# A graph layer on one core: edge products on 64 rows of the array in steps of four tiles, with the older setup, in place of products on 128 rows in steps of two

## The chip, the core and the metric

The kernel runs on one core of one Trainium2 chip. Its time is the time of one execution on the device in microseconds (us); the median of several runs is given. Five engines work side by side, each on its own queue in order: TensorE (PE, with its weight loads shown apart as PEld), VectorE (DVE), ScalarE (ACT), GpSimd (POOL, here used to issue indirect DMAs) and SyncE (SP, which issues DMAs).

## What is computed

There are 12,500 nodes with 128 features and 412,500 edges with 64 features, sorted by `dst`. With `h = relu(layernorm(x))`:

```python
h0 = h @ Wn + bn;  q = h @ Wq + bq;  k = h @ Wk + bk;  v = h @ Wv + bv
eh = edge_features @ We + be
hmid = leaky_relu(concat(q[src], k[dst], eh) @ A1 + b1, 0.2)
scores = leaky_relu(hmid @ A2 + b2, 0.2)
w = softmax(scores.mean(-1), over all edges)
out = segment_sum(w[:, None] * v[dst], src)
result = x + gamma * layernorm(h0 + out) + beta
```

## The kernel before

`A1` is folded into the weights of q, k and the edges at the start (L261 to L266), so that an edge's hidden row is a sum of three rows of 128 numbers. Edges are handled in tiles of 128; eight tiles are a group (`SUPER`), and there are 403 groups.

**Setup** (L171 to L594). The index lists `src` and `dst` are read by SP at once (L246, L248) into a pool of their own; `indices()` (L293) makes from them, on DVE, the place of each edge's source node, its block and its offset in a window of 42 nodes, and writes the offsets to DRAM (`off_d`), eight columns of tiles with one copy and one DMA (L346, L347). `nodes()` (L545) goes over the 98 node tiles in 20 groups of five: layer norm, transpose, one product with four weights into a bank, then three bf16 parts of q, k and v. The remainders between the parts are formed in PSUM, by a product with minus the identity (L579, L581). Beside it run the count of edges per block (`count`, L380) and 98 DMAs that clear the ends of the first table (`clear_ends`, L161). In all of the setup SP's queue goes in the program's order (L243); the other engines' order is the scheduler's.

**First stage** (`first_stage`, L652). For each tile it makes the rows of 128 edges: the product of the edge features with `w_ea`, and, summed into the same bank, the k and v rows of the window, picked by a 0/1 matrix `sel` made on DVE (L678). The edge features of a group come with the features of tiles 0 to 3 on partitions 0 to 63 and those of tiles 4 to 7 on partitions 64 to 127. Before the change `w_ea` is a block matrix of 128 rows and 2 x 128 columns, zero off the diagonal, so that one f32 product of 128 rows (L700) gives the edge part of tile k and of tile k+4, side by side in one bank; two bf16 products (L703) add the window's rows. One step does two tiles; a `Later` object puts off the bank's eviction by one step: ACT copies the place (L683) and the bank (L686, 128x512) into a row tile, and POOL scatters its two tiles with two indirect DMAs (L642) into a table in DRAM, ordered by the blocks of the source. PSUM has two banks for this (`ps_row`), the row tiles are seven buffers (`pr`).

**Second stage** (`second_stage`, L713). For each block of 128 source nodes it reads the block's rows back (L723), turns them on PE (L759), adds q with another 0/1 matrix (L762), takes the leaky maximum (L770 on ACT, L771 on DVE), makes scores (L779, L786, L790, L796, L808 to L831), and sums the weighted v rows on PE (L854) into `acc` (L861, L863). Its jobs stand in a plan written out by hand: each is put at a step with a fixed lag to the one that it needs.

The edges go in four chunks of 86, 121, 121 and 75 groups. While chunk c is in the first stage, chunk c-1 is in the second, the slots of chunk c+1 are worked out (`ready`: `count`, `plan`, `place_slots`, the last with the chain PE L475, DVE L519) and the table of c+1 is cleared. `interleave` takes the next step of whichever job is furthest behind, and the queues of PE, DVE, ACT and SP keep this order in the main loop (L1021). A group counts as four steps of the first stage before and after the change.

Of the kernel before, what the change touches and what calls it, by code (L numbers as in the profile page):

```python
# [10 lines left out]
FP = mybir.dt.float32  # L11
# [11 lines left out]
P = 128  # L23
# [33 lines left out]
def _ceil(a, b):  # L57
    return -(-a // b)
# [21 lines left out]
class Later:  # L80


    def __init__(self):
        self.now = 0
        self.todo = {}

    def after(self, steps, job):
        self.todo.setdefault(self.now + steps, []).append(job)

    def step(self):  # L90

        self.now += 1
        for job in self.todo.pop(self.now, []):
            job()

    def rest(self):
        while self.todo:
            self.step()
            yield


@with_exitstack
def kernel(ctx: ExitStack, tc: tile.TileContext, n_edges, x, src, dst, ea, w_nv, w_qt, w_kt,
# [71 lines left out]
    minus_b = const.tile([P, P], BF, name="minus_b")  # L175
    nc.vector.tensor_scalar(minus_b, ident, -1.0, None, op0=ALU.mult)
# [54 lines left out]
    w_ea = const.tile([P, 2, D], FP, name="w_ea")  # L231
# [11 lines left out]
    early.enter_context(tc.manual_schedule(engines={ET.SP}))  # L243
    xp = early.enter_context(tc.tile_pool(name="index", bufs=1))
    raw_src = xp.tile([P, NT], I32, name="raw_src")
    nc.sync.dma_start(out=raw_src, in_=src)  # L246
    raw_dst = xp.tile([P, NT], I32, name="raw_dst")
    nc.sync.dma_start(out=raw_dst, in_=dst)  # L248
    nc.vector.memset(w_ea, 0.0)

    with tc.tile_pool(name="prep", bufs=1) as prep, tc.tile_pool(name="prep_ps", bufs=1, space=PSUM) as pps:
# [13 lines left out]
        for b in range(2):  # L265
            nc.vector.tensor_copy(w_ea[b * DE:(b + 1) * DE, b, :], fold[b * DE:(b + 1) * DE, 2, :])  # L266
# [22 lines left out]
    np_ = early.enter_context(tc.tile_pool(name="nodes", bufs=2))  # L289
    tps = early.enter_context(tc.tile_pool(name="t_ps", bufs=2, space=PSUM))  # L290
    mps = early.enter_context(tc.tile_pool(name="m_ps", bufs=4, space=PSUM))

    def indices():  # L293
        f = xp.tile([P, NT], FP, name="f")
        nc.vector.tensor_copy(f, raw_src)
# [9 lines left out]
        nc.vector.scalar_tensor_tensor(raw_src, f, float(P), whole, op0=ALU.mult, op1=ALU.add)  # L305
        nc.scalar.dma_start(out=qrow_d, in_=raw_src)

        if t_end < NT:
# [3 lines left out]

        offset = xp.tile([P, NT], FP, name="offset")
        nc.vector.tensor_copy(offset, raw_dst)
# [4 lines left out]
        nc.tensor.matmul(t_bank[:, :NG], lhsT=ones[0:1, :], rhs=head, start=True, stop=True)  # L319
        nc.vector.tensor_sub(offset.rearrange("p (g k) -> p g k", k=SUPER),  # L320
                             offset.rearrange("p (g k) -> p g k", k=SUPER),
                             t_bank[:, :NG].unsqueeze(2).to_broadcast([P, NG, SUPER]))
# [13 lines left out]
        off_t = xp.tile([P, _ceil(NT, P), P], U8, name="off_t")  # L336
        for t0 in range(0, NT, 8 * P):
            m = min(8 * P, NT - t0)
            off_ps = tps.tile([P, 8, P], BF, name="tp")
            for j in range(_ceil(m, P)):  # L340
                w = min(P, m - j * P)
                nc.tensor.transpose(off_ps[:w, j, :], off_b[:, t0 + j * P:t0 + j * P + w], ident_b)
            j0 = t0 // P
            j = m // P
            if j > 0:
                nc.vector.tensor_copy(off_t[:, j0:j0 + j, :], off_ps[:, 0:j, :])  # L346
                nc.scalar.dma_start(out=off_d[t0:t0 + j * P, :].rearrange("(j p) e -> p j e", p=P),  # L347
                                    in_=off_t[:, j0:j0 + j, :])
            if m > j * P:
                w = m - j * P  # L350
                nc.vector.tensor_copy(off_t[:w, j0 + j, :], off_ps[:w, j, :])
                nc.scalar.dma_start(out=off_d[t0 + j * P:t0 + m, :], in_=off_t[:w, j0 + j, :])

    indices()
# [190 lines left out]
    def nodes():  # L545
        for t0 in range(0, NTN, NGRP):
# [5 lines left out]
            parts = np_.tile([P, NGRP, 3, D], BF, name="parts")  # L552
            parts2 = np_.tile([P, NGRP, 3, 2 * D], BF, name="parts2")
            for j0 in range(0, n, 4):
# [6 lines left out]
                for i in range(0, m, 2):  # L561
                    two = range(i, min(i + 2, m))
                    mp = {}
                    for j in two:
                        mp[j] = mps.tile([P, 4, D], FP, name="mp")
                        nc.tensor.matmul(mp[j].rearrange("p a d -> p (a d)"), lhsT=hT[:, j, :],
                                         rhs=w_all.rearrange("p a d -> p (a d)"), start=True, stop=False,
                                         skip_group_check=True)
                    for j in two:
                        nc.vector.tensor_add(mp[j][:, 1:4:2, :], mp[j][:, 1:4:2, :], bias_all[:, 1:4:2, :])  # L570
                        nc.vector.tensor_add(hn[:, j0 + j, :], mp[j][:, 0, :], bias_all[:, 0, :])

                    for s in range(3):
                        for j in two:
                            q, kv = parts[:, j0 + j, s, :], parts2[:, j0 + j, s, :]
                            nc.scalar.activation(kv, mp[j][:, 2:4, :], AF.Copy)
                            if s < 2:
# [74 lines left out]
    def first_stage(c):  # L652
# [28 lines left out]
        def evict(g, k, bank):  # L681
# [5 lines left out]
            for b in range(2):  # L687
                scatter(c, g, b * halves + k, row[:, b, :], sent)
# [400 lines left out]
```

## Time and profile before

| | us |
|---|---|
| median of 3 runs (6614.16 to 6650.77) | 6635.68 |
| the profiled execution's own time | 6635.68 |
| its span, from the first to the last instruction | 6634.0 |
| setup, up to the first scatter | 372 |
| chunk 0 in the first stage | 372 to 1395 |
| chunk 1 in the first stage | 1395 to 2962 |
| chunk 2 in the first stage | 2962 to 4603 |
| chunk 3 in the first stage | 4603 to 5722 |
| second stage alone | 5722 to 6490 |
| sums, layer norm, output | 6490 to 6634 |

The boundaries of the chunks are the starts of their first scatters on POOL. In the profile's rows a matmul's duration includes its way through the array, so that the matmuls of one run overlap: what one costs a full queue is the distance from one start to the next. An f32 product stands in the rows as two records, each with a weight load of its own.

### The profile page before, as it was taken

To read this page: it belongs to the slowest core of one execution; us is meant where nothing else is said; L and a number is where in the kernel's file an instruction comes from. 1 tells how busy PE (TensorE), PEld (TensorE's weight loads), DVE (VectorE), ACT (ScalarE), POOL (GpSimd) and SP (SyncE) were. 2 spreads that over 40 slices of the span, in tenths; PEclk is the share of its full clock that TensorE was granted. 3 is DMA by queue.
4 is the path that set the end of the run, shared out by engine and by line. 5 is a ranking of instruction groups with operands and counts; after the bars stand their busy time and mean duration, and the time that the engine had idled before them with its cause. 6 is when DMAs were issued, how large, how long until landed. Compare 5 with 4: busy or idle time off the path is not lost. (4 is left out here: it accounts for less than half of the span.)

```text
span 6634.0 us, 100311 instructions
## 1 busy us (share of the span) xinstructions
PE 5220.0 (79%) x32180; PEld 3524.0 (53%) x32180; DVE 4479.1 (68%) x14096; ACT 2187.9 (33%) x5896; POOL 3379.4 (51%) x3236
## 2 busy tenths in 40 slices
PE   5666655568888887878888888887999999988881
PEld 3333433245555555556556555555676767665550
DVE  8655655556666666667666666665777777777778
ACT  3432222223333333333333333333343434333331
POOL 0057677765666666656666665565555555200000
PEclk8777677778989889889999998888999999999995
DMA  6755454557777777767777777676777878544443
GB/s 191 215 169 158 136 160 153 157 183 205 221 216 222 220 214 221 218 203 230 242 246 242 238 235 229 218 230 210 247 257 254 256 257 259 186 152 152 153 141 117
DMA packets 607567, 1362.17 MB, mean 205 GB/s; under 512 B 120100, under 2 KB 336860, under 8 KB 569016
## 3 DMA queue, kind: packets, MB, share of 16 engines
q1 hardware_dynamic: 423572, 880.87, 46.3%
q0 software_dynamic: 154704, 424.26, 17.7%
q10 hardware_dynamic: 28756, 50.57, 2.4%
q8 instruction: 255, 4.18, 0.3%
q14 instruction: 280, 2.29, 0.1%
HBM read 782.14 MB, written 573.14 MB: 204 GB/s over the span
## 5 line engine op out<-in xcount | busy, mean ns | idle before, releaser
L642 POOL DMA_INDIRECT tab<-row,slots x3223 | 3377.7, 1048 | 2341.8 <-issue 807.8
L686 ACT ACTIVATE row<-row_ps 128x512 f32<-128x512 f32 x1612 | 952.3, 591 | 1421.6 <-PE row_ps L703 607.7
L700 PE MATMUL row_ps<-w_ea,ea_t 128*128 128x256 f32 x3224 | 1111.5, 430 | 121.9 <-ACT row L686 71.8
L854 PE MATMUL o_ps<-rows_of,w 128*128 128x128 f32 x7252 | 1121.3, 298 | 71.7 <-DVE w L845 48.9
L771 DVE TENSOR_TENSOR rows_of<-h_ps,low 128x512 f32<-128x512 f32 (+1 forms) x980 | 634.9, 648 | 652.9 <-ACT low L770 412.7
L845 DVE TENSOR_SCALAR w<-iota_f,rows_of,score 128x128 f32<-128x128 f32 x3626 | 1022.4, 351 | 10.6
L854 PEld LDWEIGHTS o_ps<-rows_of,w 128*128 128x128 f32 x7252 | 941.9, 199 | 119.6 <-DVE w L845 73.8
L770 ACT ACTIVATE low<-h_ps 128x512 f32<-128x512 f32 (+1 forms) x980 | 551.2, 562 | 1115.6 <-PE h_ps L762 496.0
L700 PEld LDWEIGHTS row_ps<-w_ea,ea_t 128*128 128x128 f32 x3224 | 623.6, 213 | 492.3 <-issue 205.7
L762 PE MATMUL h_ps<-sel_q,qw 128*128 128x512 bf16 (+1 forms) x2940 | 774.8, 373 | 4.6 <-DVE sel_q L750 3.3
L519 DVE TENSOR_REDUCE num<-run 128x5 f32<-128x500 f32 x646 | 433.4, 671 | 402.9 <-remote 212.9
L703 PE MATMUL row_ps<-kv,sel 126*128 126x256 bf16 x3224 | 679.3, 295 | 12.3 <-DVE sel L678 11.7
L779 PE MATMUL s_ps<-rows_of,a_sb 128*32 128x512 f32 (+1 forms) x1960 | 513.8, 625 | 126.3 <-DVE most_of L826 55.3
L759 PE MATMUL h_ps<-ident,rows_of 128*128 128x128 f32 x3626 | 589.3, 284 | 0.5 <-issue 0.5
L475 PE MATMUL run<-one,rest_b 128*128 128x500 f16 x642 | 275.3, 429 | 317.0 <-DVE num L519 240.5
L759 PEld LDWEIGHTS h_ps<-ident,rows_of 128*128 128x128 f32 x3626 | 449.7, 147 | 108.5 <-issue 83.3
L703 PEld LDWEIGHTS <-sel 126*128 126x128 bf16 x3224 | 344.0, 107 | 304.2 <-issue 73.4
L796 PEld LDWEIGHTS s_ps<-heads,z 96*128 96x128 f32 (+1 forms) x3136 | 389.3, 193 | 199.9 <-DVE z L790 142.4
L796 PE MATMUL s_ps<-heads,z 96*128 96x3 f32 (+1 forms) x3136 | 409.0, 251 | 90.8 <-DVE z L790 73.0
L786 ACT ACTIVATE z<-s_ps,b_col 64x512 f32<-64x512 f32 (+1 forms) x392 | 267.4, 682 | 615.1 <-PE s_ps L779 418.5
L468 DVE TENSOR_TENSOR one<-bins_b,block 128x500 f16<-128x500 bf16 x646 | 430.9, 667 | 0.3 <-PE run L475 0.3
L790 DVE SCALAR_TENSOR_TENSOR z<-z 64x512 f32<-64x512 f32 (+1 forms) x392 | 267.4, 682 | 203.5 <-ACT z L786 178.4
(178 smaller groups left out, 4929.0 us busy)
## 6 DMA issues: line engine op xcount, KB each, us to landing
rows_of<-tab SPq DMA_DIRECT2D x196, 1413.5 KB
ea_t<-in_ea SPq DMA_DIRECT2D x403, 256.0 KB
tab<-blank SPq DMA_DIRECT2D x392, 257.0 KB
rows_of<-tab SPq DMA_DIRECT2D x98, 1028.0 KB
rows_of<-tab SPq DMA_DIRECT2D x98, 899.5 KB
tab<-row,slots POOLq DMA_INDIRECT x3223
offs<-off_d SPq DMA_DIRECT2D x403, 126.0 KB
qw<-q_tab SPq DMA_DIRECT2D x392, 96.0 KB
```

What stands on the lines that cost most here:

```text
L642: i = nc.gpsimd.indirect_dma_start(out=tabs[c][:, :], out_offset=bass.IndirectOffsetOnAxis(ap=slots[c][t // (8 * STR)][:m, t % (8 * STR):t ...
L686: nc.scalar.activation(row[:, :, 1:ROW], bank, AF.Copy)
L700: nc.tensor.matmul(bank[:, :, 0:D], lhsT=ea_g[:, ts(k, P)], rhs=w_ea, start=True, stop=False, skip_group_check=True)
L703: nc.tensor.matmul(bank[:, b, :], lhsT=sel[:, ts(b * halves + k, P)], rhs=kv, start=False, stop=True, skip_group_check=True)
L759: nc.tensor.matmul(h_ps[:, ts(j, P)], lhsT=rows_of[i][:, q * QUAD + j, 1:D + 1], rhs=ident, is_transpose=True, start=j == 0, stop=False, s ...
L762: nc.tensor.matmul(h_ps[:, 0:m * P], lhsT=qws[i][:, ts(k, D)], rhs=plss[i][:, q * QUAD * P:(q * QUAD + m) * P], start=False, stop=k == 2, ...
L770: nc.scalar.activation(low, h_ps, AF.Copy, scale=SLOPE)
L771: nc.vector.tensor_max(rows_of[i][:, q * QUAD:q * QUAD + m, 1:D + 1], h_ps.rearrange("p (j e) -> p j e", j=m), low.rearrange("p (j e) -> p ...
L779: nc.tensor.matmul(state["s_ps"][32 * q:32 * (q + 1), 0:m * P], lhsT=a2_sb, rhs=rows_of[i][:, q * QUAD:q * QUAD + m, 1:D + 1], start=True, ...
L796: nc.tensor.matmul(state["s_ps"][:, 0:nq * QUAD].rearrange("p (q j) -> p j q", j=QUAD)[:, j, :], lhsT=state["z"][:32 * nq, ts(j, P)], rhs= ...
L845: nc.vector.tensor_scalar(w, iota_f, rows_of[i][:, t, 0:1], state["score", i][:, t:t + 1], op0=ALU.is_equal, op1=ALU.mult)
L854: nc.tensor.matmul(state["o_ps"][:, 0:D], lhsT=w, rhs=rows_of[i][:, t, D + 1:ROW], start=t == 0, stop=t == ct - 1)
```

## The change

Two parts of the kernel change together.

In the first stage the weights are one matrix of 128 columns again, on both halves of the partitions, and each tile has an f32 product of its own on 64 rows: tiles k and k+1 on the array's rows 0 to 63 into one bank, tiles k+4 and k+5 on rows 64 to 127 into the other. A step does four tiles, a `yield` follows, the two banks are evicted, and another `yield` follows. The `Later` class goes.

The setup is another one. SP's queue is left to the scheduler. `src` and `dst` are read by ACT's queue, one after the other, into one buffer in a pool that opens only when the folding of the weights is done, and that closes before the nodes' pools open. The offsets go out with one copy and one DMA for each 128 tiles. The remainders of the bf16 parts are formed in SBUF, by DVE subtractions over five tiles at a time, and ACT makes all parts. `acc` is cleared with a memset, and the first chunk adds to it in place of a copy.

```diff
-    w_ea = const.tile([P, 2, D], FP, name="w_ea")
+    w_ea = const.tile([P, D], FP, name="w_ea")
...
-    early.enter_context(tc.manual_schedule(engines={ET.SP}))
-    xp = early.enter_context(tc.tile_pool(name="index", bufs=1))
-    raw_src = xp.tile([P, NT], I32, name="raw_src")
-    nc.sync.dma_start(out=raw_src, in_=src)
-    raw_dst = xp.tile([P, NT], I32, name="raw_dst")
-    nc.sync.dma_start(out=raw_dst, in_=dst)
-    nc.vector.memset(w_ea, 0.0)
...
-        for b in range(2):
-            nc.vector.tensor_copy(w_ea[b * DE:(b + 1) * DE, b, :], fold[b * DE:(b + 1) * DE, 2, :])
+        nc.vector.tensor_copy(w_ea, fold[:, 2, :])
...
-    np_ = early.enter_context(tc.tile_pool(name="nodes", bufs=2))
-    tps = early.enter_context(tc.tile_pool(name="t_ps", bufs=2, space=PSUM))
-    mps = early.enter_context(tc.tile_pool(name="m_ps", bufs=4, space=PSUM))
-
-    def indices():
+    with tc.tile_pool(name="index", bufs=1) as xp, tc.tile_pool(name="index_ps", bufs=1, space=PSUM) as ips:
+        raw = xp.tile([P, NT], I32, name="raw")
+        nc.scalar.dma_start(out=raw, in_=src)
...
+        raw = xp.tile([P, NT], I32, name="raw")
+        nc.scalar.dma_start(out=raw, in_=dst)
...
-            if j > 0:
-                nc.vector.tensor_copy(off_t[:, j0:j0 + j, :], off_ps[:, 0:j, :])
-                nc.scalar.dma_start(out=off_d[t0:t0 + j * P, :].rearrange("(j p) e -> p j e", p=P),
-                                    in_=off_t[:, j0:j0 + j, :])
...
+                nc.vector.tensor_copy(off_t[:w, j, :], off_ps[:w, j, :])
+                nc.scalar.dma_start(out=off_d[t0 + j * P:t0 + j * P + w, :], in_=off_t[:w, j, :])
...
-                        for j in two:
-                            q, kv = parts[:, j0 + j, s, :], parts2[:, j0 + j, s, :]
-                            nc.scalar.activation(kv, mp[j][:, 2:4, :], AF.Copy)
-                            if s < 2:
-                                nc.vector.tensor_copy(q, mp[j][:, 1, :])
-                                nc.tensor.matmul(mp[j][:, 2:4, :], lhsT=minus_b, rhs=kv, start=False, stop=False,
-                                                 skip_group_check=True)
...
+                    nc.vector.tensor_add(hn[:, j0 + j, :], mp[:, 0, :], bias_all[:, 0, :])
+                    nc.vector.tensor_add(qkv[:, j0 + j, :].rearrange("p (a d) -> p a d", a=3),
+                                         mp[:, 1:4, :], bias_all[:, 1:4, :])
...
+            for s in range(3):
+                for to, of in ((parts, qkv[:, :n, 0:D]), (parts2, qkv[:, :n, D:3 * D])):
+                    if s < 2:
+                        nc.scalar.activation(to[:, :n, s, :], of, AF.Copy)
+                        nc.vector.tensor_sub(of, of, to[:, :n, s, :])
...
-    acc = ctx.enter_context(tc.tile_pool(name="acc", bufs=1)).tile([P, NTN, D], FP, name="acc")
+    acc = late.tile([P, NTN, D], FP, name="acc")
+    nc.vector.memset(acc, 0.0)
...
         for g in range(g0, g0 + n):
-            for k in range(halves):
-                later.step()
+            for k in range(0, halves, 2):
 
                 ea_g, kv, sel = got[g]
-                bank = ps_row.tile([P, 2, 2 * D], FP, name="row_ps")
-                nc.tensor.matmul(bank[:, :, 0:D], lhsT=ea_g[:, ts(k, P)], rhs=w_ea, start=True, stop=False,
-                                 skip_group_check=True)
+                banks = [ps_row.tile([P, 2, 2 * D], FP, name="row_ps") for _ in range(2)]
+                for j in range(2):
+                    for b in range(2):
+                        nc.tensor.matmul(banks[b][:, j, 0:D], lhsT=ea_g[b * DE:(b + 1) * DE, ts(k + j, P)],
+                                         rhs=w_ea[b * DE:(b + 1) * DE, :], start=j == 0, stop=False,
+                                         skip_group_check=True)
                 for b in range(2):
-                    nc.tensor.matmul(bank[:, b, :], lhsT=sel[:, ts(b * halves + k, P)], rhs=kv, start=False, stop=True,
-                                     skip_group_check=True)
-                later.after(1, lambda g=g, k=k, bank=bank: evict(g, k, bank))
+                    for j in range(2):
+                        nc.tensor.matmul(banks[b][:, j, :], lhsT=sel[:, ts(b * halves + k + j, P)], rhs=kv, start=False,
+                                         stop=True, skip_group_check=True)
                 if k == 0 and g + 2 < g0 + n:
                     load(g + 2)
-                if k == 1 and g + 1 < g0 + n:
+                yield
+                for b in range(2):
+                    evict(g, b * halves + k, banks[b])
+                if k == 0 and g + 1 < g0 + n:
                     select(g + 1)
                 yield
...
-            if c == 0:
-                nc.vector.tensor_copy(acc[:, b, :], state["o_ps"][:, 0:D])
-            else:
-                nc.vector.scalar_tensor_tensor(acc[:, b, :], acc[:, b, :], score[:, ct:ct + 1], state["o_ps"][:, 0:D],
-                                               op0=ALU.mult, op1=ALU.add)
+            nc.vector.scalar_tensor_tensor(acc[:, b, :], acc[:, b, :], state.pop(("score", i))[:, ct:ct + 1],
+                                           state["o_ps"][:, 0:D], op0=ALU.mult, op1=ALU.add)
```

## The prediction

> **What bounds the kernel now.** I read the page first, then the busy time by stage (boundaries: the first scatter of each chunk), then PE's timeline, then the waits.
>
> ```profile
> PE 5220.0 (79%) x32180; PEld 3524.0 (53%) x32180; DVE 4479.1 (68%) x14096; ACT 2187.9 (33%) x5896; POOL 3379.4 (51%) x3236
> ...
> L642 POOL DMA_INDIRECT tab<-row,slots x3223 | 3377.7, 1048 | 2341.8 <-issue 807.8
> L686 ACT ACTIVATE row<-row_ps 128x512 f32<-128x512 f32 x1612 | 952.3, 591 | 1421.6 <-PE row_ps L703 607.7
> L700 PE MATMUL row_ps<-w_ea,ea_t 128*128 128x256 f32 x3224 | 1111.5, 430 | 121.9 <-ACT row L686 71.8
> ...
> L703 PE MATMUL row_ps<-kv,sel 126*128 126x256 bf16 x3224 | 679.3, 295 | 12.3 <-DVE sel L678 11.7
> ```
>
> PE is the busiest engine, and the changed product (L700) is one of its two largest lines. ACT waits mostly for PE's L703, POOL mostly for its own issuing. By stage (columns: stretch, length, busy us of PE, PEld, DVE, ACT, POOL with counts, granted clock, DMA share, GB/s):
>
> ```profile
> 0.00:372.00 372.00, 230.37 (x1457) 121.74 (x1458) 272.71 (x875) 144.75 (x476) 1.70 (x13) 0.84 0.71 203
> 372.00:1395.00 1023.00, 616.96 (x3007) 339.75 (x3007) 600.40 (x1662) 239.69 (x691) 718.15 (x688) 0.72 0.50 154
> 1395.00:2962.00 1567.00, 1269.21 (x7606) 857.97 (x7606) 1005.84 (x3242) 528.81 (x1446) 1003.67 (x969) 0.87 0.73 215
> 2962.00:4603.00 1641.00, 1359.01 (x8637) 960.18 (x8636) 1058.21 (x3327) 573.95 (x1555) 1014.52 (x969) 0.92 0.74 231
> 4603.00:5722.00 1119.00, 1069.31 (x7119) 783.55 (x7116) 816.76 (x2636) 446.28 (x1190) 641.38 (x599) 0.99 0.79 251
> ```
>
> A scatter costs POOL 1048 ns and 251 ns of issue (807.8 us / 3223), 1.30 us. In chunk 0 that is 688 x 1.30 = 894 of 1023 us: **POOL paces it**. In chunk 3 PE is busy 1069 of 1119 us: **PE paces it**. Between them no engine is full. A busy PE counts overlapping records, so I also summed the records at their start-to-start distances and divided by the granted clock: PE's real work is 52, 71, 74 and 85% of chunks 0 to 3. The rest is waiting in a chain of engines with fixed lags.
>
> **The products, per four tiles.** At full clock L700's two records start 215 ns apart and L703's 108 (medians of start times, 1700 to 2600 and 4300 to 6500 us). Now: 2 x (2 x 215 + 2 x 108) = 1292 ns. After: four f32 products of 128 columns are eight records; records of that size (L854, 128x128 f32) start 112 ns apart. Whether the two halves of the array run beside each other is the main question. No row of before shows two row groups in turn, but two show parts of it.
>
> ```profile
> 1909.82 0.38 PE L703 MATMUL row_ps<-kv,sel 126*128 126x256 bf16 x2
> 1910.13 1.05 PE L796 MATMUL s_ps<-heads,z 64*128 64x2 f32 x8
> 1911.12 1.16 PE L854 MATMUL o_ps<-rows_of,w 128*128 128x128 f32 x8
> ```
> ```profile
> 4822.62 1.06 PE L779 MATMUL s_ps<-rows_of,a_sb 128*32 128x512 f32 x6
> 4823.61 0.29 PE L730 MATMUL t_bank<-ident,rows_of 128*11 128x128 f32 x1
> ```
>
> The second: three f32 products into different column strips, two of 512 columns and one of 384. At L700's price (215 ns for 256 columns of a record) they cost 4 x 430 + 2 x 323 = 2.37 us one after the other; the next group starts after 0.99 us. So f32 products on separate parts of the array **do overlap** here. The first prices going into a 64-row form and out: from L703 to a 64-row L796 200 ns, to a 96-row one 108; out to L854 177 against 111. That is 92 + 66 = 158 ns per visit.
>
> On this the Trainium skill, "TensorEngine Tiling (Array Packing)", Key Properties, speaks against the change: "Changing tiling mode (not just tile) drains the TensorE". The trace agrees, with the 158 ns above. By "TensorE: Matmul & The Clock Gate", Part 3, row tiles start about 4 ns apart, so that a pair would take one product's time: the overlapping sum below.
>
> - Overlapping: 92 + 4 x 111 + 66 + 4 x 108 = **1034 ns**, 258 less.
> - One after the other: 92 + 8 x 111 + 66 + 4 x 108 = **1478 ns**, 186 more.
>
> By chunk there are 172, 242, 242 and 150 steps of four tiles at clocks 0.72, 0.87, 0.92, 0.99. Overlapping, PE is spared 62 + 72 + 68 + 39 = 240 us; otherwise it pays 44 + 52 + 49 + 28 = 173. I take overlapping, since L779 is the nearest row. How much reaches the end I choose by stage: 0.15 where POOL paces, 0.35, 0.35, and 0.7 where PE does: 9 + 25 + 24 + 27 = **-85 us**. What is late next is POOL (3224 x 1.30 = 4190 of the first stage's 5350 us) and the second stage's chain with DVE.
>
> **The banks.** Each pair of banks is filled, evicted in the next half step and filled again: the distance is as before, but ACT now makes two evictions in it. The second comes 0.2 (L683, 195 ns) + 0.6 (L686) = 0.8 us later, and behind a waiting product stands all of PE's queue. Between the end of an eviction and the load of L700 that reuses its bank two steps on, the slack is 2.0 us at the median in chunk 0, 3.0 in chunks 1 and 2, 3.6 in chunk 3; about one in ten is under 0.8. The mean of what 0.8 exceeds the slack by is 41 ns; x 806 steps = **+33 us**. If a wait of that kind held nobody up, 0; if every step paid 0.8, 645.
>
> **Bursts.** Every other step gets 1034 ns of PE for 646, the one between gets none, with two evictions and four scatters (5.2 us of POOL, where a step lasts 3.0 to 3.8). Seven row buffers of two tiles cover POOL. PE's 0.39 us is the risk: answers in the second stage's chain (L796, L813, L820 with DVE between) come later in even steps. Bounds: 0 if the slack takes it up, 806 x 0.39 = 313 if every even step grows and no odd one shrinks. With a median slack of some 3 us I choose under a quarter: **+70 us**.
>
> **The setup**, up to 372 us. Removed in L700's line: only the memset of the block matrix (0.27 us). The index lists: `raw_src` and `raw_dst` are issued at 0.8 and 9.0 us and cast at 9 and 16; after, they wait for the folding's buffers (last reader L272, ending at 22.5 us, earlier without the lists ahead of it), and the second for the first's cast. The index work on DVE, which ends at 57 us, ends some 10 to 30 us later, plus 26 copies of 0.27 us for 4.0 us (+3). DMAs: 26 in place of 5 to `off_d` on ACT's queue at 0.4 us, with one buffer reused four times. Nodes per group of five on DVE: out go 5 x (L570 429 + two L578 of 284 - a 128x384 addition of 560, from L361's 128x384) = 2.2 us; in come subtractions of 640 and 1280 columns, twice each, 2 x (0.81 + 1.46) = 4.5 us, by L361's 815 ns for 640 and its slope of 1.0 ns per column; net +2.3 us, 20 groups: +47 us of DVE, which is busy 273 of 372. PE loses the minus-identity products; ACT's copies stay about as many elements. The DMA share is 0.7 to 0.8 there, so the bytes, which are the same, can hide part. SP's queue without a told order can put the 98 clearing DMAs ahead of node loads; bound 0 to 30. The memset of `acc` (at most 13.2 us, L919's row for that size) finds DVE idle before the lists land: 0, else 13. `acc`'s first sums grow by 57 ns x 98 = 6 us of DVE, busy 64% there: 0. Sum of the bounds: 0 to 120; I take 30 for the lists and 20 of the 47: **+50 us**.
>
> **The sum**, against the profiled execution's 6635.7 (1.7 around its span; it is the median too): 6635.7 - 85 + 33 + 70 + 50 = **6704 us**, +1.0%.
>
> **Rivals.**
> 1. *Faster.* PE paces all chunks: 0.7 of the 240 us counts, the bursts vanish in the slack, the setup costs half: 6635.7 - 168 + 33 + 25 = **6526**. For it: PE over 80% busy from chunk 1 on. Against: POOL at 87% in chunk 0, real work of PE near 72% in chunks 1 and 2. With the other terms as forecast (33 + 70 + 50 = 153 us) it decides from 153 / 240 = 0.64 of the spared time on.
> 2. *The halves don't overlap.* Then PE pays; of the 173 us I count 0.3, 0.5, 0.5, 0.8: +86. 6635.7 + 86 + 33 + 70 + 50 = **6875**. For it: no row with two row groups. Against: L779.
> 3. *The setup grows* to +110, DVE being full and SP's order poor, the rest as forecast: **6764**.
>
> **Chances.** Forecast (6640 to 6770) 0.42, rival 1 0.22, rival 2 0.20, rival 3 0.16. The range leaves out the lower half of rival 1 and the upper part of rival 2, about 0.2: 6540 to 6900. A measurement can tell about 0.5% (33 us) from no change; below 6602 lie 0.20 of rival 1 and 0.03 of the forecast, within 0.12 in all, above 6669 the rest: 0.23, 0.12, 0.65.
>
> **What would show it.** The 64-row records of the two halves starting a few ns apart, and four tiles in about 1.03 us of PE (1.48: rival 2). Waits of the products for L686 growing from 217 us. The first scatter near 420 us. Chunk 3 shorter, chunk 0 not. Wrong would be a first scatter by 380, or chunk 1 and 2 shorter by over 60 us each (rival 1).

## The result, and the profile after

The changed kernel takes **6944.37 us** (median of 4 runs, 6935.73 to 6959.5) beside 6633.55 us of the kernel before (4 runs, 6614.16 to 6650.77): a ratio of **1.0472**, interval [1.0435, 1.0508]. It is slower by 311 us, where 68 were forecast: 174 us above the forecast's own range (6640 to 6770 us), and 44 above the wider one that takes in the rivals (6540 to 6900). Its profiled execution took 6936.2 us with a span of 6934.5 us.

The page of the changed kernel, the lines that answer to those of before:

```profile
PE 5230.4 (75%) x35012; PEld 3411.6 (49%) x35012; DVE 4550.3 (66%) x13999; ACT 2163.0 (31%) x5624; POOL 3357.4 (48%) x3236
...
L597 POOL DMA_INDIRECT tab<-row,slots x3223 | 3355.7, 1041 | 2643.0 <-ACT row L638 904.2
L639 ACT ACTIVATE row<-row_ps 128x512 f32<-128x512 f32 x1612 | 944.2, 590 | 1462.6 <-PE row_ps L659 523.3
...
L654 PE MATMUL row_ps<-w_ea,ea_t 64*128 64x128 f32 x6448 | 724.2, 343 | 86.7 <-ACT row L639 43.6
...
L659 PE MATMUL row_ps<-kv,sel 126*128 126x256 bf16 x3224 | 580.9, 311 | 17.8 <-DMA offs<-off_d 15.1
```

The edge product's busy time fell from 1111.5 to 724.2 us, though it has twice the instructions. Single scatters and evictions cost what they did. What grew is POOL's idle time, 2341.8 to 2643.0 us, and its chief releaser is now ScalarE's row (95 us of the growth are the longer wait for the first scatter). By stage, cut again at the first scatter of each chunk (columns as in the prediction's table):

```profile
0.00:485.00 485.00, 187.93 (x1073) 92.95 (x1074) 337.36 (x778) 146.36 (x205) 1.75 (x13) 0.84 0.61 156
485.00:1552.00 1067.00, 625.36 (x3689) 318.05 (x3687) 601.08 (x1665) 223.80 (x690) 717.54 (x689) 0.65 0.47 147
1552.00:3175.00 1623.00, 1283.18 (x8583) 832.01 (x8583) 1008.00 (x3239) 525.59 (x1446) 1006.44 (x968) 0.83 0.69 208
3175.00:4857.00 1682.00, 1379.19 (x9607) 950.35 (x9605) 1058.33 (x3324) 566.31 (x1554) 1008.09 (x968) 0.89 0.72 226
4857.00:6018.00 1161.00, 1074.42 (x7710) 753.90 (x7709) 820.92 (x2643) 446.71 (x1191) 623.59 (x599) 0.99 0.76 242
```

Against before: **setup +113** (485 for 372), **chunks +44, +56, +41, +42**, together +183, and +5 behind the last scatter. No stage got shorter by more than 1 us. The granted clock of TensorE is lower in chunks 0 to 2, 0.65, 0.83 and 0.89 for 0.72, 0.87 and 0.92.

### The profile page after: what moved, and what is told of

The parts are those of the page before. It is cut to its first block, busy times and chain, and to the rows that moved or that the text cites. A ratio compares the mean times of both kernels' runs of the same rounds, so it can differ in the third digit from the quotient of the medians.

```text
span 6934.5 us, 105584 instructions
## 1 busy us (share of the span) xinstructions
PE 5230.4 (75%) x35012; PEld 3411.6 (49%) x35012; DVE 4550.3 (66%) x13999; ACT 2163.0 (31%) x5624; POOL 3357.4 (48%) x3236
## 5 line engine op out<-in xcount | busy, mean ns | idle before, releaser
L597 POOL DMA_INDIRECT tab<-row,slots x3223 | 3355.7, 1041 | 2643.0 <-ACT row L638 904.2
L811 PE MATMUL o_ps<-rows_of,w 128*128 128x128 f32 x7252 | 1135.9, 300 | 84.3 <-DVE w L802 64.9
L719 PE MATMUL h_ps<-sel_q,qw 128*128 128x512 bf16 (+1 forms) x2940 | 799.8, 383 | 0.0
L654 PE MATMUL row_ps<-w_ea,ea_t 64*128 64x128 f32 x6448 | 724.2, 343 | 86.7 <-ACT row L639 43.6
L654 PEld LDWEIGHTS row_ps<-w_ea,ea_t 64*128 64x128 f32 x6448 | 536.8, 224 | 501.1 <-issue 342.9
L736 PE MATMUL s_ps<-rows_of,a_sb 128*32 128x512 f32 (+1 forms) x1960 | 544.4, 639 | 144.3 <-DVE most_of L783 73.2
L716 PE MATMUL h_ps<-ident,rows_of 128*128 128x128 f32 x3626 | 608.8, 290 | 0.9 <-issue 0.9
L659 PE MATMUL row_ps<-kv,sel 126*128 126x256 bf16 x3224 | 580.9, 311 | 17.8 <-DMA offs<-off_d 15.1
L435 PE MATMUL run<-one,rest_b 128*128 128x500 f16 x642 | 298.0, 464 | 384.5 <-DVE num L479 264.2
L719 PEld LDWEIGHTS <-qw 128*128 128x128 bf16 x2940 | 302.5, 103 | 129.6 <-issue 23.6
```

The lines of the kernel that those rows point to most:

```text
L597: i = nc.gpsimd.indirect_dma_start(out=tabs[c][:, :], out_offset=bass.IndirectOffsetOnAxis(ap=slots[c][t // (8 * STR)][:m, t % (8 * STR):t ...
L654: nc.tensor.matmul(banks[b][:, j, 0:D], lhsT=ea_g[b * DE:(b + 1) * DE, ts(k + j, P)], rhs=w_ea[b * DE:(b + 1) * DE, :], start=j == 0, stop ...
L659: nc.tensor.matmul(banks[b][:, j, :], lhsT=sel[:, ts(b * halves + k + j, P)], rhs=kv, start=False, stop=True, skip_group_check=True)
L716: nc.tensor.matmul(h_ps[:, ts(j, P)], lhsT=rows_of[i][:, q * QUAD + j, 1:D + 1], rhs=ident, is_transpose=True, start=j == 0, stop=False, s ...
L719: nc.tensor.matmul(h_ps[:, 0:m * P], lhsT=qws[i][:, ts(k, D)], rhs=plss[i][:, q * QUAD * P:(q * QUAD + m) * P], start=False, stop=k == 2, ...
L736: nc.tensor.matmul(state["s_ps"][32 * q:32 * (q + 1), 0:m * P], lhsT=a2_sb, rhs=rows_of[i][:, q * QUAD:q * QUAD + m, 1:D + 1], start=True, ...
```

## Two things that the trace shows at once

**The halves of the array do overlap.** One step of the changed kernel on TensorE (start, length, line, tile, count):

```profile
5203.22 0.94 PE L811 MATMUL o_ps<-rows_of,w 128*128 128x128 f32 x6
5204.08 0.71 PE L654 MATMUL row_ps<-w_ea,ea_t 64*128 64x128 f32 x8
5204.73 0.61 PE L659 MATMUL row_ps<-kv,sel 126*128 126x256 bf16 x4
5205.18 0.49 PE L716 MATMUL h_ps<-ident,rows_of 128*128 128x128 f32 x3
```

Eight records take 0.65 us to the next line; they start in pairs 7 ns apart (median of the last chunk), one record of each half. In that chunk such a step takes 1095 ns at the median, and TensorE comes to it 204 ns after a record that else is followed after 111: 1095 + 93 = 1188 ns for four tiles. Before's two steps of two tiles take 2 x 656 = 1312. So 124 ns are spared, not 258: besides the 93 on the way in, the first pair and the last take 213 and 210 ns where the others take 112.

**The setup waits behind its own clearing.** SyncE's queue in the first 200 us of the changed kernel:

```profile
5.79 0.33 SPq L229 DMA_DIRECT2D col<-in_cols  x1
6.23 160.23 SPq L144 DMA_DIRECT2D tab<-blank  x98
167.88 0.34 SPq L618 DMA_DIRECT2D ea_t<-in_ea  x1
181.85 13.40 SPq L509 DMA_DIRECT2D xt<-in_x  x3
```

All 98 clearing transfers go out in one piece, ahead of the first node load, which comes at 181.85 us for 22.54 before; the DMA share is 1.00 in the first 150 us for 0.67 before. The index lists share the DMA engines with them, and are cast at 37.73 and 62.53 us, where before's were at 9 and 16 (VectorE, same kernel):

```profile
37.73 1.84 DVE L261 CAST f<-raw 128x3224 f32<-128x3224 int32 x1 [18.23 <-DMA raw<-in_src]
...
62.53 1.84 DVE L283 CAST offset<-raw 128x3224 f32<-128x3224 int32 x1 [15.47 <-DMA raw<-in_dst]
```

## The experiments

Each run is compared with before beside it on the same chip. Before itself took 6031 to 6037 us in four series of these runs (e1 to e4, e9 to e12, e15 and e16, e17 and e18) and 6628 and 6734 us in two (e5 to e8; e13 and e14), though it is the same program; ratios are therefore only taken within a series. The pair of 6031 (e1 to e4) and 6628 us comes from one chip, by the record's number. What differs is taken up with e13 and e14.

| run | what | before | ratio [95%] |
|---|---|---|---|
| e1 | loop alone | 6031 | 1.0062 [1.0040, 1.0084] |
| e2 | setup alone | 6031 | 1.0184 [1.0161, 1.0206] |
| e3 | steps of four, old products | 6031 | 1.0091 [1.0063, 1.0119] |
| e4 | PE spared, nothing else | 6031 | 1.0004 [0.9992, 1.0016] |
| e5 | the whole change | 6628 | 1.0464 [1.0421, 1.0507] |
| e6 | the same, SP's order told | 6628 | 1.0364 [1.0326, 1.0403] |
| e7 | after's node rows alone | 6628 | 1.0004 [0.9984, 1.0024] |
| e8 | loop alone, evictions apart | 6628 | 1.0395 [1.0359, 1.0432] |
| e9 | loop alone | 6032 | 1.0072 [1.0048, 1.0095] |
| e10 | steps of four, old products | 6032 | 1.0083 [1.0056, 1.0109] |
| e11 | PE spared | 6032 | 1.0005 [0.9989, 1.0020] |
| e12 | plain row writes | 6032 | 1.1278 [1.1252, 1.1303] |
| e13 | loop alone | 6734 | 1.0270 [1.0242, 1.0299] |
| e14 | steps of four, old products | 6734 | 1.0370 [1.0342, 1.0398] |
| e15 | 64-row products, steps of two | 6037 | 1.0163 [1.0143, 1.0184] |
| e16 | evictions in pairs alone | 6037 | 1.0067 [1.0047, 1.0086] |
| e17 | evictions in pairs alone | 6031 | 1.0080 [1.0064, 1.0097] |
| e18 | PE spared | 6031 | 1.0003 [0.9992, 1.0013] |

### Parts of the change

Loop alone (e1): before's setup with after's `first_stage`, `evict` and `w_ea`. Setup alone (e2): the other way round. e3 is before with steps of four tiles and its own products:

```diff
-            for k in range(halves):
-                later.step()
+            for k in range(0, halves, 2):
...
-                later.after(1, lambda g=g, k=k, bank=bank: evict(g, k, bank))
+                yield
+                for j in range(2):
+                    evict(g, k + j, banks[j])
```

e4 spares TensorE a quarter of each edge product:

```diff
-  nc.tensor.matmul(bank[:, :, 0:D], lhsT=ea_g[:, ts(k, P)], rhs=w_ea, ...
+  nc.tensor.matmul(bank[:, :, 0:96], lhsT=ea_g[:, ts(k, P)], rhs=w_ea[:, :, 0:96], ...
```

> The setup of before with the first stage of after (products of 64 rows, steps of four tiles). In the trace of after the setup was 113 us longer and the four chunks 183 us together. If the two parts simply add up, this gives 6634 + 183 = about 6820 us, with the first scatter at 372 us as before. If the loop's loss is only an effect of the late setup, it gives under 6680 us.

> The setup of after with the first stage of before (block matrix of 128 rows, steps of two). If the parts add up: 6634 + 113 = about 6747 us, first scatter near 485 us, the chunks as long as before. If the loop's loss is an effect of the late setup: over 6880 us.

> Before, with one edit: steps of four tiles, evicted half a step later, but with the products of 128 rows of before (same PE work as before, two banks a step). Theory of the bursts: the products of each step filled PE's waits for DVE and the other engines, and in fours they fill only every other one; then this is as slow as the first stage of after or slower, since it also lacks the spared PE time: 6820 to 6900 us. Rival, that the 64-row form itself costs (its entries and exits, the lower granted clock): this stays within 30 us of before, 6604 to 6664 us.

> Before, with the edge products on 96 of the 128 columns of each tile, so that a quarter of the hidden columns gets no edge features: it spares PE 2 x 55 ns for each two tiles, 177 us at full clock, about 200 at the granted clock, which is what the overlapping products of after spare (192 ns for four tiles by its trace), with no other change in steps. If PE's time is worth what I took (a third to 0.7 of it), 6634 - 70 to 140 = 6495 to 6565 us. If spared PE time only turns into waits, 6614 to 6650 us.

Measured: loop +37 us, setup +114 us (first scatter at 474 for some 366), steps of four +59, TensorE spared +1, which is none. So e3 lies between its two expectations, and e4 meets its second. Here the time spared in e4 is worth nothing. In the first two chunks its waits say why (engine, line and what it waited for; us in total, times, longest):

```profile
ACT row L683 <- DMA tab<-row,slots: 1031.9, 549, 5.8
```

ScalarE waits for row buffers that the scatters have not given back yet: GpSimd paces. By chunk these waits are 581.5, 431.8, 18.6 us and none, so this holds for chunks 0 and 1 only. The last chunk, in which the prediction let 0.7 of the spared time through, takes 1079 us for 1091 in e2, which has before's loop, and 1087 and 1094 when e4 is repeated (e11, e18): nothing clear there either, and no run shows what bounds it. The record spacing of the narrow product is 163 ns for 216, so it was truly spared. The setup's cost agrees with the +113 of the result; the loop's, 37, does not agree with +183.

### The setup's loss

e6 is the changed kernel with one line more; e7 is before with after's `nodes` body (one addition into SBUF and subtractions on VectorE, no products with minus identity).

```diff
+    early.enter_context(tc.manual_schedule(engines={ET.SP}))
```

> The whole change, timed on the chip that runs the experiments. On the chip of the result it cost 311 us: first scatter +113, the four chunks +44, +55, +42, +42, the tail +5. Theory A (the cost of the loop depends on the chip: where the chunks are paced by the answers of one engine to another the bursts cost more): if this chip is again the one on which before takes about 6031 us, the sum of the two parts measured there, 37 for the loop and 114 for the setup, so 1.025 (1.020 to 1.030) of before, about 6182 us, and chunks that grow by 60 us at most together. Theory B (the two parts don't add: the loop costs more behind the late setup): 1.035 or more, with the chunks +100 or more. On a chip where before takes about 6634 us: 1.047 by both.

> After, with the order of SP's queue told again as before (one line), all else as after. Theory T (the setup's loss is SP's queue: 98 clearing transfers ahead of everything, so that the index lists, the writes of off_d and the node loads crawl behind them): the first scatter comes 80 to 110 us earlier than in after, and the whole is 1.3 to 1.8% under after. Theory N (it is the 47 us of subtractions on VectorE, and the lists that go through ScalarE's queue with one buffer): the first scatter comes at most 50 us earlier, 0.8% at most.

> Before, with after's way of splitting the node rows alone: one addition of the biases to a 128x384 block in SBUF and subtractions there on VectorE, in place of products with minus identity in PSUM. All else is before, the told order of SP and the index lists too. Theory T: VectorE finds room, the first scatter comes 0 to 25 us later than 366, 1.000 to 1.004. Theory N: it comes 35 to 60 us later, 1.006 to 1.010.

e5 met a before of 6628 us and confirms the result (chunks +44, +43, +53, +33 over before's profile). In e6 SyncE's queue mixes the clearing with the loads again:

```profile
6.35 1.04 SPq L144 DMA_DIRECT2D tab<-blank  x2
7.44 0.45 SPq L619 DMA_DIRECT2D ea_t<-in_ea  x1
```

The first scatter comes at 408 us for 488 in e5: 80 of the setup's 113 us are SyncE's order (theory T at its lower end); the whole gains 0.9% (60 us, its chunks together take 28 us longer than e5's), less than the 1.3 expected. e7 is even with before, first scatter at 374: VectorE's extra work in the node rows is **hidden** in before's setup, and this half of theory N falls. The 36 us between 408 and 372 remain for the other half, the lists through ScalarE's queue and the single `off_t` buffer, and for the setup's smaller edits; no run parted these.

### The loop: evictions apart

e8 is the loop alone with bank 0 evicted as the next half step begins and bank 1 half a step later:

```diff
-                for b in range(2):
-                    evict(g, b * halves + k, banks[b])
+                evict(g, k, banks[0])
...
+                evict(g, halves + k, banks[1])
```

> Before's setup and after's first stage (the loop alone, which took 1.0062 of before on the chip with before at 6031 us), with the two banks of a step evicted apart: the first right after the next half step begins, the second half a step later, ahead of the next step's products, so that ScalarE makes one eviction and GpSimd two scatters in each half step as before, while TensorE still gets four tiles at once. Theory E (the cost lies in the pairs of evictions and in four scatters at once): it is gone, 1.000 to 1.002. Theory P (it lies in TensorE's own burst of four tiles, behind which the second stage's products stand): it stays, 1.005 to 1.008; and the second eviction, now just ahead of the products that need its bank's pair, can add a wait, up to 1.015.

1.0395 lies outside both expectations, which were made for the other kind of run. Chunks 0 to 2 are as in e5 (1065, 1603, 1705 us for 1067, 1610, 1694), the last is longer, 1219 for 1152. So spreading the evictions while TensorE still gets four tiles at once recovers nothing on balance. That doesn't clear the pairs of evictions: the edit brings a wait of its own, as its expectation allowed. The products wait 377 us for evictions, and 141 in e5 with the same loop and the evictions together. The waits of e8:

```profile
PEld row_ps L697 <- ACT row L682: 223.6, 187, 5.3
...
PE row_ps L697 <- ACT row L682: 153.3, 122, 4.8
```

### The same kernels beside 6031 and beside 6734 us

> The loop alone again (before's setup, after's first stage). In the runs where before takes 6031 us it cost 37 us, while in the profiles where before takes about 6630 us the loop of the whole change costs 173 to 202 us, and there PE's, ACT's and DVE's semaphore updates come late: while scatters run, 20 to 54% of them come over 0.5 us after the instruction's modelled end, against 0 to 1% in the profiles beside 6031 us. If these runs are again of the late kind (before at about 6630), theory L (a step whose two banks are filled together and emptied together passes PE -> ACT -> PE once per step with nothing in between, and so pays each late answer in full): 1.025 to 1.035 with chunks +150 to +220. Theory T (the tiled products themselves): the same time, but the next kernel would not have it. Beside 6031 us: 1.006 again.

> Steps of four tiles with the 128-row block products of before, again. Theory L: with late semaphore updates it costs as much as the loop with tiled products or a little more, 1.025 to 1.045, since the steps and banks are the same and PE is not spared. Theory T: within 0.01 of before, as beside 6031 us, where it cost 59 us (1.009).

> Before with the edge product on 96 of 128 columns (a quarter of the hidden columns' edge features are left out), again: PE spared, nothing else changed. If spared PE time is worth nothing here either: 0.997 to 1.003. If the prediction's weights hold (about a third of what is spared): 0.990 to 0.995.

> The loop alone a third time, to meet the kind of run in which before takes about 6630 us and semaphore updates come late while scatters run. There, 6634 x 1.025 to 1.035 (chunks +150 to +220 together) by both theories of the loop's loss; beside 6031 us, 1.007 again, and nothing new.

> Steps of four tiles with before's block products, a third time. Beside 6630 us: theory L (the steps of four tiles cost more where answers come late, whatever the products are): 1.025 to 1.045. Theory T (the products in two row halves cost it, by their changes of form or their twice as many instructions): 1.000 to 1.012. Beside 6031 us: 1.008 again.

e9 to e11 met the 6031 us again and repeat e1, e3 and e4. e13 and e14 met the other kind and settle the question between theory L (the steps cost it) and theory T of these runs (the 64-row products cost it): the loop alone costs **178 us**, the steps of four tiles with before's own products **251 us**. The steps cost it, and the 64-row products, with the other pairing of tiles in a row buffer that goes with them, give 73 us back. T falls.

What the two kinds are can be read from one kernel in both, the steps of four tiles. By stage, the four chunks, beside 6032 us (e10) and then beside 6734 us (e14); columns as before:

```profile
368.00:1314.00 946.00, 630.74 (x3091) 338.47 (x3089) 607.88 (x1682) 241.47 (x697) 719.70 (x689) 0.75 0.52 166
1314.00:2635.00 1321.00, 1159.99 (x7421) 797.72 (x7524) 993.33 (x3225) 536.23 (x1438) 998.53 (x969) 0.94 0.85 256
2635.00:4040.00 1405.00, 1276.53 (x8534) 923.23 (x8639) 1052.59 (x3324) 576.46 (x1555) 1024.55 (x968) 0.96 0.86 270
4040.00:5172.00 1132.00, 1068.63 (x7012) 777.13 (x7112) 818.76 (x2641) 448.49 (x1190) 628.99 (x599) 0.99 0.78 248
```

```profile
373.00:1442.00 1069.00, 599.15 (x3021) 334.46 (x3019) 600.03 (x1661) 236.01 (x690) 718.86 (x688) 0.74 0.48 147
1442.00:3112.00 1670.00, 1295.51 (x7497) 871.00 (x7596) 1003.34 (x3244) 534.87 (x1445) 1000.92 (x969) 0.85 0.69 202
3112.00:4837.00 1725.00, 1381.35 (x8535) 969.23 (x8640) 1052.65 (x3326) 572.44 (x1555) 1016.58 (x968) 0.90 0.71 220
4837.00:6076.00 1239.00, 1110.83 (x7014) 795.82 (x7114) 819.67 (x2642) 447.80 (x1189) 620.99 (x599) 0.97 0.71 226
```

DVE, ACT and POOL are busy equally long with equally many instructions; the setup (368 and 373 us) and the stretch behind the last scatter (915 and 913) are equal too. Only the chunks grow, by waits. The granted clock isn't the reason: it is lower in chunks 1 and 2 of e14, but chunks 0 and 3 grow by 123 and 107 us at nearly the same clock. The waits of e10, then of e14:

```profile
PEld L475 <- issue: 276.5, 293, 20.9
```

```profile
POOL tab L642 <- ACT row L682: 956.5, 341, 12.6
...
PEld L475 <- issue: 544.3, 350, 14.2
...
ACT row L685 <- remote: 342.2, 88, 14.8
...
DVE num L519 <- remote: 247.7, 49, 10.7
DVE score L808 <- remote: 232.3, 46, 10.0
```

"remote" is a semaphore that moved when no recorded instruction that raises it had just ended; e10 has no such row among its 190 largest waits. One such wait in e14's order of time:

```profile
4023.41 0.95 PE L796 MATMUL s_ps<-heads,z 96*128 96x3 f32 x8
...
4024.22 1.14 PE L854 MATMUL o_ps<-rows_of,w 128*128 128x128 f32 x8
...
4024.76 0.14 DVE L807 COPY score<-most_of 128x1 f32<-128x1 f32 x1
...
4025.91 0.96 POOL L642 DMA_INDIRECT tab<-row,slots  x1 [0.30 <-issue]
...
4032.43 0.17 DVE L808 TENSOR_TENSOR score<-s_ps,none 128x11 f32<-128x11 f32 x1 [7.54 <-remote]
...
4032.86 0.37 PE L813 MATMUL s_ps<-ident,top_of 128*1 128x128 f32 x1 [7.50 <-DVE top_of L810]
```

VectorE waits for the scores of L796, whose records end at 4024.4, and gets word 8 us later; TensorE stands 7.5 us behind it. GpSimd scatters on meanwhile.

I then took every instruction of PE, DVE and ACT that raises a semaphore and measured from its recorded end to the semaphore's next event. In e10 it is 8 to 13 ns at the median, and at most 1% take over 0.5 us. In e14, of PE's some 52, 52, 44 and 32% in chunks 0 to 3 do, of DVE's 40, 32, 31 and 22, of ACT's 44, 32, 33 and 28; **0% in the setup and behind the last scatter**. The profile of before that the prediction was made from is of this kind (PE 54, 51, 45, 28%), and so is the changed kernel's. There, in the chunks, some 40% of the updates are late when their instruction ends within a run of scatters (less than 0.4 us apart), by 1.1 us in the mean over all, and 10% (0.2 us) otherwise.

### Attempts to part it further

e12 writes the rows by plain transfers on ScalarE's queue to consecutive slots; e15 keeps before's steps of two with 64-row products; e16 and e17 empty before's two banks together; e18 repeats e4.

```diff
# e12, in scatter
-            i = nc.gpsimd.indirect_dma_start(out=tabs[c][:, :], out_offset=..., in_=row[:m, :], in_offset=None)
+        nc.scalar.dma_start(out=tabs[c][at * P:(at + 1) * P, :], in_=row)
# e15: banks = ps_row.tile([P, 2, 2, 2 * D]) once for all steps
-                bank = ps_row.tile([P, 2, 2 * D], FP, name="row_ps")
+                bank = banks[:, :, k % 2, :]
+                for b in range(2):
+                    nc.tensor.matmul(bank[:, b, 0:D], lhsT=ea_g[b * DE:(b + 1) * DE, ts(k, P)], ...
# e16, e17
-                later.after(1, lambda g=g, k=k, bank=bank: evict(g, k, bank))
+                full.append((k, bank))
+                if k % 2 == 1:
+                    for j, it in full:
+                        evict(g, j, it)
```

> Before with the rows written to consecutive slots by plain transfers on ScalarE's queue instead of scatters by GpSimd (it leaves out where each row belongs, so sums go to wrong nodes; as many bytes are written and read, and the plan of the slots is still worked out). If GpSimd's scatters make the semaphore updates late: none of them is late any more, POOL no longer paces, and chunks 0 to 2 shrink to 85 to 95% of before's in the late kind, near those of the runs beside 6031 us or below. If the traffic or the rest of the loop makes them late, a third of the updates stays late and the chunks stay near 1023, 1568 and 1640 us, plus ACT's issuing of 3224 transfers.

> Products of 64 rows in the lower and upper array rows, each half into its own bank, but in before's steps of two tiles: one tile over two banks, its slots used in turn (even half steps the first slot of both banks, odd ones the second), one eviction of 128x512 half a step later, as before; setup of before. PE is spared less, since each half step changes form: 92 + 2 x 111 + 66 + 2 x 108 = 596 for 646 ns, 50 ns per two tiles, about 90 us of PE over 1612 steps at the granted clock. Theory L (what costs is the step of four tiles, with half steps that have no product): no loss is left, 0.994 to 1.002 in both kinds of run. Theory C (each change of form drains TensorE, which waits for late answers more the oftener it happens): 1.004 to 1.02 beside 6630 us, as many changes again as in the loop alone (1612 instead of 806).

> Before with TensorE's steps of two tiles as they are, but both banks evicted together at the end of every second half step (at once for the second bank, not half a step later). If TensorE's burst of four tiles is what costs: 1.000 to 1.01. If the two evictions and four scatters together cost, or that a bank is emptied with no slack before its next product: 1.02 to 1.05 beside 6630 us and 1.005 to 1.02 beside 6031 us.

> Evictions in pairs with TensorE's steps of two tiles, again. Beside about 6630 to 6730 us: if TensorE's four tiles at once are what costs the 251 us of the steps of four, 1.000 to 1.012; if emptying the banks together does, 1.025 to 1.045. Beside 6031 us, 1.006 again, and it stays open which of the two it is where answers come late.

> Before with the edge product on 96 of 128 columns (a quarter of the hidden columns' edge features are left out), again. Beside about 6630 to 6730 us: some 3224 x 2 x 54 ns at full clock, about 390 us of PE's records at the granted clock, are spared; at the 73 us in about 240 that the 64-row products gave back there, 0.975 to 0.99; if sparing is worth nothing without the bursts, 0.997 to 1.003. Beside 6031 us, 1.000 again.

All of these met a before of about 6031 us, where no update is late.

- e12 says nothing on the late updates: there were none to remove, and ScalarE's queue spends 1353 us issuing 3224 transfers, with the second stage's work behind them. A miss.
- e15 costs 96 us, more than either expectation allowed for in this kind of run, and it isn't a fair test of the changes of form: the products now wait for evictions of the same tile. Its waits, together 1339 us:

```profile
PEld row_ps L700 <- ACT row L685: 900.6, 894, 4.9
...
PE row_ps L700 <- ACT row L685: 438.8, 426, 4.4
```

  In e4 the same two are 464 and 269 us, none of it in the last chunk; in e15 200 us fall there, and some 80 of the 96 us that it costs (that chunk takes 1172 us for 1091 in e2, with before's loop).

- e16 and e17: pairing the evictions alone costs 46 and 51 us, nearly the 52 to 59 us of the steps of four tiles (e3, e10). But the two costs fall in different chunks, so one cause for both is not shown (length of each chunk in us, beside 6031 to 6037 us):

| | chunk 0 | 1 | 2 | 3 |
|---|---|---|---|---|
| before's loop (e2) | 936 | 1325 | 1407 | 1091 |
| loop alone (e1) | 938 | 1323 | 1410 | 1119 |
| steps of four (e3) | 945 | 1327 | 1409 | 1135 |
| evictions in pairs (e16) | 936 | 1337 | 1428 | 1108 |

  The steps of four lose their time in the last chunk, the pairs in chunks 1 to 3, and they have a wait of their own: the second bank's eviction stands right behind its products, so that ScalarE waits for TensorE. The waits of e16, then of e2:

```profile
ACT row L686 <- PE row_ps L702: 1035.6, 675, 10.1
```

```profile
ACT row L665 <- PE row_ps L682: 381.8, 272, 12.7
```

  e16's 1.0067 lies in both of its expectations, and e16 was not measured beside 6630 us. Which part of a step of four tiles costs, TensorE's burst or the emptying of both banks together, is open in both kinds.
- e18: 1.0003; a quarter of the edge product spared is worth nothing beside 6031 us, for the third time.

## Why the prediction was wrong, step by step

- **What bounds the kernel.** Too kind a reading. I took the rest between the engines' work as "a chain of engines with fixed lags". The lags aren't fixed: in before's own waits stood these rows, which I passed over:

```profile
PEld L475 <- issue: 407.2, 307, 16.5
...
ACT row L686 <- remote: 329.7, 74, 10.6
...
DVE rows_of L771 <- issue: 228.9, 157, 5.4
DVE num L519 <- remote: 212.9, 42, 12.0
```

  Nor did GpSimd alone pace chunk 0, as I read it. In all of before ScalarE waited 27.4 us for a free row buffer, and in chunk 0 GpSimd waited 97 us for ScalarE's rows; where GpSimd does pace, in e2 with the same loop beside 6031 us, ScalarE waits 995.1 us, 581 of them in chunk 0. Before, then e2:

```profile
ACT row L683 <- DMA tab<-row,slots: 27.4, 22, 3.6
```

```profile
ACT row L662 <- DMA tab<-row,slots: 995.1, 527, 6.4
```

- **Products, -85 us: near in size, in part by luck.** The halves overlap, so rival 2 (6875) is wrong, though its time lies nearer than the forecast's. What is spared per four tiles is 124 ns, not 258, since form changes cost some 290 ns per step in place of 158; 240 us become about 115. Of these 73 us reached the end (e14 less e13), 0.63 of them, where the weights let 0.35 through: half the saving and nearly twice the share cancel. By chunk e13 is 11 us longer than e14 in chunk 0 and 19, 30 and 46 shorter in the others: the weights' order was right. The term also kept before's clock, and the 64-row products come with a lower one in chunk 0 (0.65 in the changed kernel and in e13, 0.74 in e14); what that is worth no run shows. Chunk 3, which was to get shorter, grew by 42 us.
- **Banks, +33, and bursts, +70: the step that failed.** Together 103 were forecast, e14 shows 251: the waits that steps of four tiles add were put too low by 148 us, the largest part of the miss. The bound of 313 us for the bursts held it; the choice "with a median slack of some 3 us ... under a quarter" didn't. A median slack says little where a third of the answers come over 0.5 us late, and these by 2.6 us in the mean (the changed kernel's chunks). That this is why the steps cost more is argued from the two kinds of run, not tested by itself. The sign by which I meant to see the banks was wrong as well: the products' waits for evictions fell from 217 to 119 us, and it is POOL that runs dry: its waits for ScalarE's two copies into the row are 1334 us for 1095 together, 904 for 391 at the place and 430 for 704 at the bank. Where no answers are late the same steps cost 52 to 59 us, about half of the 103.
- **Setup, +50: mis-sized, 113.** "Bound 0 to 30" for SyncE's order, which had no working, was the failed term: it is 80 (e6). The 20 of VectorE's 47 us are 0 (e7). The lists got 30, against 36 left over for them and the smaller edits. I had weighed the 98 transfers by the place of the loads in the queue and not by the bytes ahead of everything else: a DMA share of 1.00 for 150 us. Rival 3's sum of +110 was right, for half of its reason.
- **The sum as measured:** 6633.6 - 73 + 251 + 113 = 6925 us for 6944.4; the 20 us left lie within the intervals. The terms come from three series with different befores, so that they add up so well is not a test of each.

Open: which part of a step of four tiles costs so much where updates are late (TensorE's burst, the paired evictions, or both in one chain), what makes the updates late beside 6630 us and not beside 6031 us, and whether TensorE's time alone is worth anything there. That the scatters delay the updates is the trace's correlation, not an experiment.

## What to carry to other kernels

Before a change takes slack out of a chain of engines, read the waits that have no releaser ("issue", "remote") on several engines: here they stood for answers that come late, and a median of the slack was then no guide. A saving on the busiest engine may be worth little (none of e4's beside 6031 us, 73 of some 115 us here); cutting the same product without any other edit shows that in one run. And whoever removes a told order of a queue should count the bytes that the scheduler may put ahead of the first load.

## What was not expected of the hardware

- The same program on the same chip takes 6031 us at one time and 6628 at another. Durations of single instructions are equal (e2 and e7: the scatter 1052 and 1047 ns, the eviction 586 and 590); what differs are semaphore updates, 14 ns after a product's recorded end at the median in one, over 0.5 us in a quarter to a half of them in the other, and only in the chunks, where GpSimd scatters.
- 64-row f32 products into the two row halves start 7 ns apart, and each change into that form and out costs about 93 + 101 + 99 ns (the way in, the longer first pair, the longer last pair). The Trainium skill, "TensorEngine Tiling (Array Packing)", Key Properties, has it that a change of tiling mode drains TensorE; the trace agrees as far as starts around such a change lie further apart, by this much, and this kept half of the spared time from being spared.
